# A first-layer product in seven half-block products, masks and bias by accumulating transfers, heads in two pairs: a two-layer graph attention network

## The chip, the cores and the metric

One core of a Trainium2 chip runs the whole kernel. The metric is the device time in microseconds of one execution; every run here is listed as being in the fast state. Before the change the median of the first three runs is 2880.1 us (2879.95 to 2880.22). Ratios of two kernels are the mean time of one kernel's fast runs over that of the other's in the same rounds on the same chip, so they are not quite the ratio of the medians quoted beside them.

## The reference, cut to what matters

32 graphs of 512 nodes with 512 features each. Per graph: normalise and rectify, a first attention layer with four heads of 256 features, ELU, a second layer with one head of 512 features, and the residual.

```python
def gat_layer(x, mask, W, a_src, a_dst, bias, concat):
    xl = (x @ W).reshape(B, N, H, F)
    asrc = jnp.einsum('bnhf,hf->bnh', xl, a_src)
    adst = jnp.einsum('bnhf,hf->bnh', xl, a_dst)
    e = jax.nn.leaky_relu(asrc[:, :, None, :] + adst[:, None, :, :], 0.2)
    e = jnp.where(mask[..., None], e, NEG_INF)
    attn = jax.nn.softmax(e, axis=1)                  # over the sources
    out = jnp.einsum('bsdh,bshf->bdhf', attn, xl)     # the "product over the sources"
    ...
    return out + bias
h = jax.nn.elu(gat_layer(h, mask, W1, att_src1, att_dst1, b1, concat=True))
return x + gat_layer(h, mask, W2, att_src2, att_dst2, b2, concat=False)
```

Each layer is a projection (`x @ W`) and, per head, a product over the sources with the attention weights p.

## The kernel before

All is in fp32. Three of the four large products already use seven half-block products in place of eight: both projections and the second layer's product over the sources. (Two matrices cut into 2 x 2 blocks need eight block products; with sums of blocks made before, and sums of results after, seven are enough.) The first layer's product over the sources is still plain, 4 source tiles of 512 columns for each of 8 blocks of features:

```python
def gather1(b, soft):
    for h in range(H):
        pk, p = soft.p.pop(h)
        for f in range(FPH):
            g = h * FPH + f
            bk, ps = banks.take()
            for s in range(NT):
                v, vkeys = features(b, h, s)
                pe(vkeys + [pk + (s,)], [bk], 0.862,
                   [(mm, (ps, v[:, f * P : (f + 1) * P], p[:, s, :]), ...)])
            act(0.62, ..., e, ps, AF.Exp, bias=b1_sb[:, 0, g : g + 1], scale=-1.0)   # ELU
            act(0.62, ..., e, e, AF.Relu, bias=1.0, scale=-1.0)
            dve(0.67, ..., nc.vector.scalar_tensor_tensor, h1[:, g, :], ps, ...)
```

VectorE makes the logits of p, adds the mask (a large negative number, bf16, in SBUF), and ScalarE exponentiates:

```python
for u in range(NT):                       # Soft.second: one head
    dve(0.67, ..., nc.vector.scalar_tensor_tensor, p[:, u, :], rr[:, 0, :], ...)
    dve(0.59, ..., nc.vector.tensor_add, p[:, u, :], p[:, u, :], m[:, u, :])
    act(0.62, ..., p[:, u, :], p[:, u, :], AF.Exp, bias=z[:, 2, j, u : u + 1])
...
dma(256e3, (), halves, xr, x[b, d * P : (d + 1) * P, :])                  # residual
dve(0.59, [xk, "b2"], halves, nc.vector.tensor_add, xr, xr, b2_sb)        # + bias
```

One thing matters more than it seemed to: no instruction is issued where it stands in the code. Each becomes a job with an assumed cost, what it reads and what it writes, and `Program.order()` works out one fixed order for each engine, and for each queue that issues transfers, from those costs. The program is emitted in that order, and nothing in it changes a list by what really finishes when.

## Time and profile before

| | before |
|---|---|
| time, median | 2880.1 us |
| span of the profiled execution | 2877.3 us |
| TensorE busy | 2842.6 us, 99% |
| VectorE, ScalarE busy | 2469.7 us (86%), 2206.1 us (77%) |
| TensorE idle between 200 and 2700 us | none |
| transfer engines busy | 38% |

These are the groups of instructions that the change touches (line, engine, operation, what it writes and reads, shape and count, then busy us, mean ns of one, and the engine's idle time before them):

```profile
L285 PE MATMUL mm<-p,xl 128*128 128x512 f32 x2016 | 871.4, 592 | 1.6 <-ACT p L274 1.6
L277 DVE TENSOR_TENSOR p<-p,m 128x512 f32<-128x512 f32 x640 | 416.4, 684 | 0.0
L277 DVE TENSOR_TENSOR xr<-xr,b_sb 128x512 f32<-128x512 f32 x124 | 84.2, 684 | 1.0 <-DMA xr<-in_x_dram 1.0
```

The first is the plain product (31 graphs of 64 records, and the last graph's second layer). The other two are VectorE's mask and bias sums, 500 us of its busy time.

### The profile page before, as it was taken

Reading aid. Unit: us, or ns where it says so; the run is one execution under the profiler, and the core shown is the slowest. Engines: PE = TensorE matmul, PEld = TensorE weight load, DVE = VectorE, ACT = ScalarE, POOL = GpSimd, SP = SyncE. Lnnn points to the kernel's source line nnn. Section 1 sums busy time; section 2 is a strip of 40 time slices with the busy share of each in tenths; the row PEclk is TensorE's granted clock in tenths of the full one; section 3 lists DMA queues with packets and bytes.
Section 4 is the critical chain, followed back from the end, with each engine's and each line's share of the span. In section 5 each row is a group of like instructions: output and inputs, shape, how many; then the busy total and the mean of one; then the engine's idle time right before and its main releaser. Section 6 shows DMA issues by size and latency. Waiting matters only on the chain.

```text
span 2877.3 us, 35818 instructions
## 1 busy us (share of the span) xinstructions
PE 2842.6 (99%) x11016; PEld 2091.4 (73%) x11016; DVE 2469.7 (86%) x5979; ACT 2206.1 (77%) x4381; POOL 54.5 (2%) x38
## 2 busy tenths in 40 slices
PE   7899999999999999999999999999999999999999
PEld 6577778777777777787777877777877778777776
DVE  6998899888888888888888888888988888988886
ACT  5878887778877788777888778787787887878872
POOL 0000000000000000000000000000000000000000
PEclk9999999999999999999999999999999999999999
DMA  6333433434333434334333334333343433434322
GB/s 199 91 102 94 128 107 102 119 96 129 106 110 112 119 99 124 103 108 121 103 117 104 109 112 119 105 113 109 107 129 91 126 107 106 123 100 110 114 70 88
DMA packets 323328, 318.71 MB, mean 111 GB/s; under 512 B 219840, under 2 KB 223936, under 8 KB 323136
## 3 DMA queue, kind: packets, MB, share of 16 engines
q1 hardware_dynamic: 323136, 316.42, 37.7%
q8 instruction: 87, 1.43, 0.2%
q14 instruction: 105, 0.86, 0.1%
HBM read 232.53 MB, written 34.54 MB: 93 GB/s over the span
## 4 chain that ended last, share of the span: by engine, by line
PE 97%; DVE 2%; ACT 0%; DMA 0%; issue 0%; SPq 0%; DVEq 0%; ACTq 0%
PE mm L285 97%; DVE p L277 1%; DVE xr L277 0%; DVE l L277 0%; DMA w_sb<-in_L_gnn_W_dram 0%; DVE xl L277 0%; ACT xr L274 0%; DVE h L277 0%; SPq L280 0%; ACT p L274 0%; DVE w_sb L277 0%; ACT ht L274 0%; DVE x L277 0%; DVE stats L277 0%; ACT l L274 0%
## 5 line engine op out<-in xcount | busy, mean ns | idle before, releaser
L285 PE MATMUL mm<-p,xl 128*128 128x512 f32 x2016 | 871.4, 592 | 1.6 <-ACT p L274 1.6
L285 PEld LDWEIGHTS mm<-p,xl 128*128 128x128 f32 x2016 | 382.4, 190 | 472.3 <-issue 413.7
L285 PE MATMUL mm<-w_sb,hs 128*128 128x257 f32 (+1 forms) x3024 | 685.8, 381 | 4.3 <-DVE hs L277 4.3
L285 PEld LDWEIGHTS mm<-w_sb,hs 128*128 128x128 f32 x3024 | 575.2, 190 | 89.5 <-DVE hs L277 4.7
L274 ACT ACTIVATE xl<-mm 128x258 f32<-128x258 f32 (+2 forms) x752 | 286.9, 382 | 420.6 <-PE mm L285 407.4
L274 ACT ACTIVATE l<-l,low 128x512 f32<-128x512 f32 x640 | 456.8, 715 | 114.3 <-DVE low L277 113.6
L274 ACT ACTIVATE p<-p,z 128x512 f32<-128x512 f32 x640 | 433.3, 713 | 72.2 <-DVE p L277 71.5
L285 PE MATMUL mm<-w_sb,h 128*128 128x257 f32 x2056 | 469.5, 380 | 7.5 <-DVE h L277 7.5
L285 PE MATMUL mm<-w_sb,ht 128*128 128x258 f32 x2112 | 475.1, 381 | 1.8 <-DVE xr L277 1.8
L277 DVE SCALAR_TENSOR_TENSOR p<-rr,z 128x512 f32<-128x512 f32 x640 | 456.1, 743 | 20.3 <-DMA rr<-drr 14.5
L285 PEld LDWEIGHTS mm<-w_sb,ht 128*128 128x128 f32 x2112 | 401.2, 190 | 73.1 <-issue 11.0
L274 ACT ACTIVATE l<-as,z 128x512 f32<-128x512 f32 x640 | 438.4, 714 | 12.5 <-DMA as<-das 7.6
L277 DVE CUSTOM_DVE_ANT_1 l<-l,mt 128x512 f32<-128x512 f32 x640 | 426.0, 682 | 14.9 <-ACT l L274 14.7
L285 PEld LDWEIGHTS mm<-w_sb,h 128*128 128x128 f32 x2056 | 390.1, 190 | 66.5 <-DVE h L277 8.3
L277 DVE TENSOR_TENSOR p<-p,m 128x512 f32<-128x512 f32 x640 | 416.4, 684 | 0.0
L277 DVE TENSOR_TENSOR xl<-xl,mm 128x258 f32<-128x258 f32 x558 | 230.3, 418 | 65.4 <-PE mm L285 51.6
L277 DVE SCALAR_TENSOR_TENSOR h<-mm,b_sb,xr 128x512 f32<-128x512 f32 x256 | 187.2, 744 | 110.3 <-ACT xr L274 110.0
L277 DVE TENSOR_TENSOR xr<-mm,xr 128x256 f32<-128x256 f32 (+1 forms) x424 | 172.1, 419 | 25.6 <-PE mm L285 22.3
L285 PE MATMUL mm<-xl,p 128*128 128x256 f32 (+1 forms) x752 | 181.0, 390 | 3.2 <-ACT p L274 3.2
L274 ACT ACTIVATE xr<-mm,b_sb 128x512 f32<-128x512 f32 x256 | 170.5, 675 | 12.3 <-PE mm L285 9.5
L285 PEld LDWEIGHTS mm<-xl,p 128*128 128x128 f32 x752 | 142.5, 190 | 32.0 <-issue 7.5
L274 ACT ACTIVATE ht<-x 128x1024 uint16<-128x1024 uint16 x124 | 159.2, 1341 | 1.2 <-PE mm L285 1.2
(92 smaller groups left out, 1977.6 us busy)
## 6 DMA issues: line engine op xcount, KB each, us to landing
rr<-drr SPq DMA_DIRECT2D x160, 512.0 KB
x<-in_x_dram SPq DMA_DIRECT2D x129, 256.0 KB
adj<-in_adj_dram SPq DMA_DIRECT2D x128, 256.0 KB
as<-das SPq DMA_DIRECT2D x64, 512.0 KB
xr<-in_x_dram SPq DMA_DIRECT2D x124, 256.0 KB
out_dram<-xr SPq DMA_DIRECT2D x124, 256.0 KB
as<-das SPq DMA_DIRECT2D x32, 256.0 KB
drr<-rr SPq DMA_DIRECT2D x160, 4.0 KB
```

Of the source, the lines that this page charges most:

```text
L274: prog.add("ACT", cost, reads, writes, lambda: nc.scalar.activation(*a, **k))
L277: prog.add("DVE", cost, reads, writes, lambda: f(*a, **k))
L285: f(*a, **k)
```

## The change

Its intent is to take an eighth of the last plain product off TensorE. The half-block products need sums of blocks, on VectorE, which has no room for them by the prediction's count (76.3 us busy per graph of 88.2, and 19.1 to be added); so the masks and the bias go to transfers that add to what is in SBUF. The heads go in two pairs with half of the next graph's projection between them, so that three buffers of p are enough. The ordering was reworked as well (12 rounds, each backwards and then forwards, in place of one; transfers now queue up one after another in the backward pass too). The core of the diff, cut:

```diff
-    DMA_LEAD, DMA_TAIL, DMA_RATE = 1.2, 1.0, 230e3
+    DMA_LEAD, DMA_TAIL, DMA_RATE = 1.2, 1.0, 280e3
...
+    ROUNDS = 12
+        for _ in range(self.ROUNDS):
+            back = self.backwards(rank)
+            start, done = self.forwards(late)      # keep the order with the earliest end
...
+    def accumulate(size, reads, writes, to, at, cost=0.95):
+        prog.add("POOL", cost, reads, writes,
+            lambda: nc.gpsimd.dma_start(to, at, accum_op=OP.add), 1.4 * size)
...
+            here = self.b == B - 1 or self.layer == 1 and (h in HERE or self.b == 0 and h < H - 1)
-                dve(0.59, ..., nc.vector.tensor_add, p[:, u, :], p[:, u, :], m[:, u, :])
+            if not here:
+                for us in (0, 1), (2, 3):          # two tiles of p a transfer
+                    accumulate(500e3, keys + [mk], keys, *(... for t in (p, md)))   # md: masks in DRAM
...
+        op(0.34, add, s1, a21, a22)                # sums1: eight block sums of one head
+        op(0.59, sub, t1, b12, b11)
+        op(0.34, sub, s2, s1, a11)
+        op(0.59, sub, t2, b22, t1)
+        op(0.34, sub, s4, a12, s2)
+        op(0.34, sub, a21, a11, a21)
+        op(0.59, sub, b12, b22, b12)
+        # and, before the last product: op(0.59, sub, b21, b21, t2)
...
+            if n in (1, 4, 5, 6):                  # gather1: seven products of a head
+                act(COPY, [bk], [key], to, ps, AF.Copy)
+            else:
+                dve(ADD, [bk, key], [key], nc.vector.tensor_add, to, to, ps)
...
+            accumulate(256e3, [xk], halves, xr, rows_of(b2, P))      # residual: bias
...
+            gather1(s, 0)                          # the loop over graphs
+        s.second(2); s.second(3); ...
+            for _ in range(14):
+                next(ahead)                        # half the projection of graph i + 2
+            gather1(s, 1)
```

Graphs 0 and 1 stay plain (`PLAIN = 1`).

## The prediction

> **What bounds the kernel now.** I first read the page's first and fourth parts, busy time by engine and the chain that ended last.
>
> ```profile
> PE 2842.6 (99%) x11016; PEld 2091.4 (73%) x11016; DVE 2469.7 (86%) x5979; ACT 2206.1 (77%) x4381; POOL 54.5 (2%) x38
> PE 97%; DVE 2%; ACT 0%; DMA 0%; issue 0%; SPq 0%; DVEq 0%; ACTq 0%
> q1 hardware_dynamic: 323136, 316.42, 37.7%
> ```
>
> The tensor engine carries 97% of the chain; VectorE has 14% of the span free, and the transfers use 37.7% of their engines. The table by stretches, cut into three times 88.2 us, says whether that holds inside the steady state and what one graph costs:
>
> ```profile
> 1000.00:1088.20 88.20, 88.20 (x346) 65.15 (x345) 77.94 (x190) 70.10 (x141) 1.01 (x1) 1.00 0.41 117
> 1088.20:1176.40 88.20, 88.20 (x345) 65.16 (x344) 76.55 (x184) 68.74 (x138) 1.38 (x1) 1.00 0.37 111
> 1176.40:1264.60 88.20, 88.20 (x345) 65.17 (x344) 74.34 (x177) 67.34 (x132) 2.58 (x1) 1.00 0.37 111
> ```
>
> Columns after the window: its length, then busy us of PE, weight loads, VectorE, ScalarE, GpSimd, then granted clock and transfer share. Nothing stalls PE: 88.2 of 88.2 us at full clock, 345 matmul records each. The code gives 344 per graph (each fp32 matmul shows as two records): 112 for each of the two projections in seven products, 56 for the second product over sources, 64 of 512 columns for the first. VectorE takes 76.3 us per graph on average, ScalarE 68.7. All the PE waits of the run together are 30.9 us, in the first 165 us and before the very last product; the rest is solid matmul. So only PE's own instruction time counts, as long as the others keep up.
>
> A record's duration (592 ns) is not its cost; matmuls overlap. The cost is the step from start to start, which runs of equal records in the timeline give:
>
> ```profile
> 1379.44 20.76 PE L285 MATMUL mm<-p,xl 128*128 128x512 f32 x48
> 1407.36 5.38 PE L285 MATMUL mm<-w_sb,hs 128*128 128x258 f32 x24
> 2833.60 3.62 PE L285 MATMUL mm<-x,ht 128*128 128x256 f32 x16
> ```
>
> 512 columns: (20.76 - 0.592)/47 = 0.429 us. 256 columns: (3.62 - 0.379)/15 = 0.216. 258: (5.38 - 0.383)/23 = 0.217. Check: 64 x 0.429 + 112 x 0.2175 + 112 x 0.217 + 56 x 0.216 = 88.2 us, the period.
>
> The same must be done for VectorE, whose durations also overlap:
>
> ```profile
> 1399.97 0.68 DVE L277 TENSOR_TENSOR hs<-hs,ht 128x512 f32<-128x512 f32 x1
> 1400.57 0.69 DVE L277 TENSOR_TENSOR ht<-ht 128x512 f32<-128x512 f32 x1
> 1401.17 0.74 DVE L277 SCALAR_TENSOR_TENSOR h<-mm,b_sb,xr 128x512 f32<-128x512 f32 x1
> ...
> 1414.52 0.42 DVE L277 TENSOR_TENSOR xl<-xl,mm 128x258 f32<-128x258 f32 x1 [0.26 <-PE mm L285]
> 1414.86 0.69 DVE L277 TENSOR_TENSOR xr<-xr,b_sb 128x512 f32<-128x512 f32 x1
> ```
>
> A 512-element sum steps by 0.60 us (1399.97 to 1400.57 to 1401.17) though shown as 0.68; a 256-element one by 0.34. ScalarE's copy of a block out of an accumulator, from the same timeline (1409.59 us minus the start before it at 1409.32), steps by 0.27 to 0.28.
>
> [...] 0.429 is 2 x 0.216 less 3 ns, so splitting 512 columns in two costs almost nothing[...]. [...]
>
> **The change part by part.**
>
> *Matmuls removed.* For graphs 2 to 31 (graphs 0 and 1 stay plain) the first product of a head becomes seven half-block products of 2 source tiles by 256 columns: 7 x 2 x 2 records, 112 per graph for four heads, instead of 64 of 512. 64 x 0.429 = 27.46; 112 x 0.216 = 24.19; 3.27 us saved per graph, 30 graphs: 98 us, all on the chain. The period falls from 88.2 to 84.9. If nothing else stalls: 2880 - 98 = 2782. Weight loads: 2091 + 30 x 48 x 0.19 = 2365 us of 2782, 85%, hidden as now.
>
> *VectorE removed, per graph.* Mask sums: 4 heads and the second layer, 4 each, 20 x 0.60 = 12.0. Bias sums into the residual: 4 x 0.60 = 2.4. Together 14.4.
> *VectorE added, per graph.* Block sums of a head: four of 256 elements, four of 512: 4 x 0.34 + 4 x 0.60 = 3.76, four heads: 15.0. Of the seven results of a head three are added by VectorE: 12 x 0.34 = 4.1. Together 19.1. Net +4.7: 76.3 becomes 81.0 us of an 84.9 us period, 95%. So the "masks by transfer" part doesn't speed anything up by itself; it makes room for the sums, and not quite enough.
> *ScalarE.* Four copies per head, 16 x 0.28 = 4.5 per graph; the ELU's exponential reads SBUF instead of an accumulator, eight times, perhaps 0.06 less each by the Relu's step of 0.52 against 0.58. 68.7 becomes 72.7 of 84.9, 86%.
> *GpSimd and transfers.* 608 of the 640 mask sums become 304 transfers (two tiles each), and 124 bias sums become 124; with the author's 0.95 us of issue, 428 are about 400 us on an engine 2% busy. Transfers: 316 MB in 37.7% of 2877 us is 292 GB/s while busy. A mask transfer writes 0.52 MB[...]: 1.8 us if only writes count, about 3.6 us if the read-back counts fully; 304 of them are 550 to 1090 us, so the share rises to 57 to 77%. [...]
> *Order.* Heads come in pairs, with 14 products of the next graph's projection (56 x 0.2175 = 12.2 us) between them. There are three buffers for p: head 2's stands free during the first pair, head 3 must reuse one of the pair's. [...] Half the buffer is released at the last seventh product, 3.4 us before the pair's end, and the sums are wanted only after four products of the next pair. [...]
>
> Sum: 2880 - 98 = 2782 as the floor. What I add is a choice: VectorE at 95% in strict static order won't always deliver block sums, or the add that frees an accumulator (wanted within two to three products of 0.86 us), in time. I allow 0.5 us of PE stall per graph, 16 us in all: 2798. Start and end I leave as they are (about 31 us of waits).
>
> **Rivals.** (1) *VectorE becomes the bound.* For: 95% on average, and the pair stage alone asks 2 x 3.76 + 6 x 0.34 + 4 x 0.67 = 12.2 us of it in 56 x 0.216 = 12.1 us of PE. Against: PE doesn't wait at all at 87%, the order is searched twelve times, and its assumed costs (0.59, 0.34) match the measured steps. If 2 us per graph leak: 2782 + 60 = 2842, within 2%. (2) *The accumulating transfers are late*: the chain gets a transfer of unknown latency where a 0.60 us sum stood. If each takes 9 us[...], head 3's chain misses by perhaps 2 us per graph, again about 2840. For: three p buffers only, and a queue shared with broadcasts. Against: the transfer engines would still be idle a quarter of the time, and today's broadcasts make VectorE wait only 14.5 us in the whole run. (3) *Seven products cost more than six eighths suggest*: if a group of two accumulating matmuls left bubbles, the gain would shrink. Against: the second product already runs such groups of 256 columns, at 0.216 us. (4) *All hidden*: PE stays solid, 2775 to 2785.
>
> **Range and chances.** Faster by over 2% means below 2822.5 us, which leaves 40 us for stalls over the floor, 1.3 us per graph. The author's tuned model and today's solid PE make that likely; the 4 us of VectorE slack makes it uncertain. 2775 to 2838 should hold 8 in 10. Faster 0.80, within 2% 0.17, slower 0.03: for slower the transfers would have to cost 5 us per graph.
>
> **What would show it.** The first product as about 3360 records of 256 columns stepping by 0.216; PE busy about 2745 us in a span near 2795; period 84.9 to 85.5; VectorE 93 to 95%; ScalarE about 85%; transfer share 57 to 77%; p<-p,m sums down to 32. PE waits should name VectorE's block sums or ScalarE's exponentials of p, under 20 us beyond the start. I am wrong if those waits exceed 45 us, if VectorE's busy time falls (then I mis-sized the sums), or if the matmul step is above 0.22.

## The result, and the profile after

The changed kernel takes 2860.94 us in the median (2858.04 to 2869.5, four runs), before 2880.16 on the same chips; the ratio is 0.9937, 95% interval 0.9916 to 0.9959. It gives the right result. It is 0.6% faster, so within 2% of before; 2798 us had been predicted, and 2860.94 lies above the predicted range of 2775 to 2838.

The page after the change, its parts on busy time, the chain and the queues:

```profile
PE 2774.1 (97%) x12456; PEld 2365.5 (83%) x12456; DVE 2584.4 (90%) x6567; ACT 2306.4 (81%) x4861; POOL 416.7 (15%) x466
PE 5%; DVE 4%; ACT 1%; DMA 1%; issue 0%; SPq 0%; DVEq 0%; POOL 0%; ACTq 0%; POOLq 0%
q1 hardware_dynamic: 327600, 332.68, 41.7%
q0 software_dynamic: 61632, 191.92, 30.3%
p<-dm POOLq DMA_DIRECT2D x304, 512.0 KB, 5.1
```

TensorE still leads in busy time, but its share of the chain fell from 97% to 5%: the chain now hops between engines and transfers and could be followed back only to about 2513 us, so its shares cover only the end. The last line gives the mask transfers' median time from issue to landing, 5.1 us. In the table by stretches, the long middle of the two kernels, before and then after:

```profile
200.00:2700.00 2500.00, 2500.00 (x9766) 1850.95 (x9765) 2168.86 (x5195) 1954.79 (x3887) 48.77 (x28) 1.00 0.38 111
```

```profile
200.00:2700.00 2500.00, 2463.33 (x11257) 2131.79 (x11256) 2311.36 (x5831) 2079.82 (x4385) 388.20 (x429) 1.00 0.75 191
```

TensorE was solid for 2500 us and now stands idle for 36.7. The count says more than the busy time. A graph is now 392 records in 84.9 us if nothing stalls, so 11,543 would fit into 2500 us; 11,257 ran. The 286 missing ones, at 84.9/392 = 0.217 us, are 62 us lost. (In before 2500 us hold 9751 records of a period of 88.2 us with 344, and 9766 ran: nothing lost.) A second count agrees: in the trace's records of the middle, the times from start to start exceed the steps by 61 us in all (before: 1.5), 44 of them in 47 waits of over 0.3 us. The step itself did not change; in the timeline of after, 16 records of 256 columns show the same 3.62 us as before:

```profile
1015.12 3.62 PE L333 MATMUL mm<-p,xl 128*128 128x256 f32 x16
1018.57 3.62 PE L333 MATMUL mm<-t,hs 128*128 128x256 f32 x16
```

So the ledger is this. Counting all matmul records by their steps (0.429, 0.2175, 0.217 and 0.216 us for 512, 258, 257 and 256 columns): before 2080, 3600, 3584 and 1736 records, 2828 us; after 160, 3600, 3584 and 5096, 2730 us. The saving is 98 us, as predicted. Everything else took 2877 - 2828 = 49 us before and 2856 - 2730 = 126 us after. Of these 77 us more, 62 lie in the middle, and some 15 at the start and the end.

What TensorE waited for in the middle, from the view of waits (total us, times, longest):

```profile
PE mm L333 <- DVE hs L319: 13.1, 5, 3.6
PE mm L333 <- DVE xr L319: 11.8, 17, 2.3
PE mm L333 <- ACT xl L316: 5.7, 12, 0.9
PE mm L333 <- ACT h L316: 5.0, 6, 1.8
```

Which matmuls they hold up is told by the groups of instructions, over the whole run:

```profile
L333 PE MATMUL mm<-xl,hs 128*128 128x256 f32 x232 | 60.8, 391 | 12.5 <-DVE xr L319 11.8
L333 PE MATMUL mm<-x,hs 128*128 128x256 f32 x464 | 110.3, 393 | 10.8 <-DVE hs L319 10.8
L333 PE MATMUL mm<-p,xl 128*128 128x256 f32 x1920 | 447.8, 381 | 6.4 <-ACT p L316 3.5 <-ACT h L316 2.9
L333 PE MATMUL mm<-t,hs 128*128 128x256 f32 x960 | 218.3, 380 | 1.2 <-ACT h L316 0.9 <-DVE t L319 0.3
L333 PE MATMUL mm<-p,hs 128*128 128x256 f32 x480 | 113.8, 380 | 1.2 <-ACT h L316 1.2
```

The first two are of the second layer's product, which was in seven products before; the last three are the new seven products. So most of the waiting is not in the new products: of the 44 us in the middle, 28 lie in the second layer's product, 10 in the projections and 6 in the new products.

None of the waits names a transfer, and `hs` are the block sums, which look like VectorE's load. One must ask what VectorE waited for in turn. The longest of the five waits for `hs`, in the timeline, line by line (start, length, engine, instruction, in brackets the idle time before it and what ended it):

```profile
446.76 0.86 POOL L327 DMA_DIRECT2D p<-dm  x1 [0.45 <-issue]
...
456.26 1.33 ACT L316 ACTIVATE p<-p,z 128x512 f32<-128x512 f32 x2 [0.99 <-DMA p<-dm]
...
457.63 0.69 DVE L319 TENSOR_TENSOR hs<-p 128x512 f32<-128x512 f32 x1 [1.29 <-ACT p L316]
...
458.38 1.22 PE L333 MATMUL mm<-x,hs 128*128 128x256 f32 x2 [3.63 <-DVE hs L319]
```

The mask transfer issued at 446.76 landed just before 456.26, 9.5 us later; ScalarE idled for it, then VectorE for ScalarE, then TensorE for VectorE. VectorE is the name on the wait, and a transfer stands at its head. But ScalarE idled for the transfer for only 0.99 us, so in this place at most about 1 of TensorE's 3.63 us is shown to be the transfer's. A wait for `xr` runs the same way with a bias transfer at its head, and there the transfer accounts for 2.00 of 2.34 us:

```profile
1159.62 0.42 DVE L319 TENSOR_TENSOR xr<-mm,xr 128x256 f32<-128x256 f32 x1 [2.00 <-DMA xr<-in_L_gnn_b_dram]
...
1160.10 1.13 PE L333 MATMUL mm<-xl,hs 128*128 128x256 f32 x4 [2.34 <-DVE xr L319]
```

In the middle the mask transfers took 4.1 to 9.7 us to land (one of 13.1 us was issued at 158 us, in the start). And the long wait goes with a lower clock: in the 50 us that hold the 3.63 us wait, the granted clock (the figure before the transfer share) is 0.97 where it was 1.00:

```profile
450.00:500.00 50.00, 46.13 (x204) 39.13 (x204) 42.99 (x112) 40.73 (x80) 9.21 (x10) 0.97 0.82 204
```

That is 0.03 x 50 = 1.5 us more. The clock record of this trace has stretches at half clock, single ones of 3.4 us (and 6.8 or 10.2 us at start and end). Four of them lie in the middle, and they go with the waits of 3.63, 3.00, 2.72 and 2.34 us: each begins within 1.3 us of the end of one, and the 16 records there take 5.25, 5.35, 5.41 and 5.30 us where 16 took 3.62. None goes with the wait of 2.29 us that ends at 1469.46. Together the four cost about 7 of the 62 us.

### The profile page after: what moved, and what is told of

Its sections match the earlier page's. It is cut to its first block, busy times and chain, and to the rows that moved or that the text cites. A ratio compares the mean times of both kernels' runs of the same rounds, so it can differ in the third digit from the quotient of the medians.

```text
span 2856.2 us, 41534 instructions
## 1 busy us (share of the span) xinstructions
PE 2774.1 (97%) x12456; PEld 2365.5 (83%) x12456; DVE 2584.4 (90%) x6567; ACT 2306.4 (81%) x4861; POOL 416.7 (15%) x466
## 3 DMA queue, kind: packets, MB, share of 16 engines
q1 hardware_dynamic: 327600, 332.68, 41.7%
q0 software_dynamic: 61632, 191.92, 30.3%
## 5 line engine op out<-in xcount | busy, mean ns | idle before, releaser
L333 PE MATMUL mm<-w_sb,hs 128*128 128x257 f32 (+1 forms) x3024 | 693.2, 383 | 19.4 <-ACT xl L316 10.8
L327 POOL DMA_DIRECT2D p<-dm x304 | 267.5, 882 | 2032.1 <-DVE p L319 1034.3
L333 PE MATMUL mm<-p,xl 128*128 128x256 f32 (+1 forms) x2016 | 489.5, 391 | 6.4 <-ACT p L316 3.5
L333 PE MATMUL mm<-w_sb,ht 128*128 128x258 f32 x2112 | 481.5, 382 | 2.2 <-ACT xl L316 1.2
L319 DVE TENSOR_TENSOR xl<-xl,mm 128x258 f32<-128x258 f32 x558 | 224.8, 417 | 36.6 <-PE mm L333 28.7
L316 ACT ACTIVATE h<-mm 128x256 f32<-128x256 f32 x480 | 175.4, 379 | 84.2 <-PE mm L333 82.0
L316 ACT ACTIVATE xr<-h,b_sb 128x512 f32<-128x512 f32 x240 | 171.5, 723 | 77.3 <-DVE h L319 76.8
L333 PE MATMUL mm<-t,hs 128*128 128x256 f32 x960 | 218.3, 380 | 1.2 <-ACT h L316 0.9
L333 PEld LDWEIGHTS mm<-t,hs 128*128 128x128 f32 x960 | 183.1, 191 | 27.0 <-ACT h L316 1.3
L319 DVE SCALAR_TENSOR_TENSOR h<-h,b_sb,xr 128x512 f32<-128x512 f32 x240 | 175.9, 745 | 20.0 <-ACT xr L316 19.2
```

Of the source, the lines that this page charges most:

```text
L316: prog.add("ACT", cost, reads, writes, lambda: nc.scalar.activation(*a, **k))
L319: prog.add("DVE", cost, reads, writes, lambda: f(*a, **k))
L327: lambda: nc.gpsimd.dma_start(to, at, accum_op=OP.add), 1.4 * size,
L333: f(*a, **k)
```

## The kernel's own plan

Since every engine is given a fixed list, the loss can be split with the builder's own arithmetic: `order()` ends with a planned time for its order. That is a calculation from its cost table, not a measurement; it was read out after the prediction.

```
             planned end   TensorE work in the plan   planned TensorE idle   measured   measured - planned
before         2863.9            2819.9                     44.0              2880.1        16
after          2787.4            2712.8                     74.6              2860.9        74
```

The plan assumes slightly short matmul steps: 2828 - 2820 = 8 us of the excess before and 2730 - 2713 = 17 us after are only that. What remains are stalls that the plan doesn't have: 8 us before, 56 us after. So the 98 us saved were lost in two ways: 31 us because the order that was found already leaves TensorE idle for that much longer, and some 48 us because execution doesn't keep to it. 98 - 31 - 48 = 19, the gain measured.

Two theories for the second loss. **T**: transfers land later than the order assumes (it counts on 5.6 to 9.0 us for a mask transfer, 5.7 in the median). **V**: VectorE, at 90% and more, can't deliver whatever the transfers do.

## The experiments

Each kernel is the changed one with the edit shown (left out: lines that only set up or clear a tile, and `ROUNDS = 40` in e6, e7 and e10). "Middle loss" is worked out as above from the count of matmul records between 200 and 2700 us; after: 62 us. The strongest comparisons are those in which the order of every instruction is the same: the first three against the changed kernel, and e7 against e4.

**e1: small mask transfers, same order.** Wrong result on purpose. (A first form without the constant exponent overflowed in the check before the chip and was not run.)

```diff
-  *(t[:, us[0] : us[-1] + 1].rearrange("p t n -> p (t n)") for t in (p, md)),
+  *(t[:, us[0], :16] for t in (p, md)),
-  p[:, u, :], p[:, u, :], AF.Exp, bias=z[:, 2, j, u : u + 1],
+  p[:, u, :], p[:, u, :], AF.Exp, bias=six[:, u : u + 1], scale=1e-6,    # six: -6.0
```

> Wrong result on purpose. The changed kernel with the same order of every instruction, but each of the 304 accumulating mask transfers moves 16 columns instead of 1024, and the exponentials of p take a constant bias so that nothing overflows. VectorE's work is untouched. Theory T (transfers land later than the fixed order assumes, and the waits reach TensorE): 2790 to 2815 us, the mask transfers land in 2 to 3 us instead of 5.1, ScalarE's waits for broadcasts and masks (177 us now) fall under 60. Theory V (VectorE at 90 to 95% can't deliver the block sums in time whatever the transfers do): 2845 to 2862 us, with the same TensorE waits for block sums and residual adds.

Measured: 2826.62 us (2823.59 to 2829.33), ratio 0.9816. 34 us are gone, more than half of the 56, with VectorE's work unchanged; the mask transfers landed after 2.4 us in the median (2.2 to 5.5). It fell between the two ranges. So the mask transfers cost that much in this order. Not separated: their own landing, and the load that they put on other transfers (the transfer engines fell from 75% to 53% busy in the middle, the bias transfers from 5.8 to 5.3 us). Its middle, and VectorE as busy as ever:

```profile
200.00:2700.00 2500.00, 2481.00 (x11392) 2160.26 (x11391) 2343.04 (x5891) 2109.78 (x4450) 390.27 (x430) 1.00 0.53 132
```

11,392 records: 151 short, 33 us lost instead of 62. The part of the expectation on ScalarE's waits was wrong: its waits for masks vanished (63.2 us in the middle before), but those for the broadcasts of the source scores only fell from 92.8 to 79.8 us.

**e2: small block sums, same order.** Wrong result on purpose.

```diff
-  dve(cost, u[1] + v[1], to[1], f, to[0], u[0], v[0])
+  dve(cost, u[1] + v[1], to[1], f, *(q[0][:, :1, :32] for q in (to, u, v)))
```

> Wrong result on purpose. Same order, same transfers, but the eight VectorE block sums of each head in the seven-product first layer work on 32 columns instead of 256 or 512, which takes about 12 us per graph of 80 off VectorE. Theory V: 2790 to 2810 us, VectorE near 78% busy. Theory T: 2840 to 2860 us, TensorE waits hardly changed, since the broadcasts and masks land as late as before.

Measured: 2859.44 us (2854.96 to 2866.13), ratio 0.9932, no different from the changed kernel.

```profile
200.00:2700.00 2500.00, 2459.13 (x11226) 2129.49 (x11225) 2005.44 (x5808) 2073.56 (x4371) 389.76 (x429) 1.00 0.75 190
```

VectorE fell from 2311 to 2005 us busy in the middle, 10.7 us per graph, and TensorE lost 69 us there instead of 62. V falls as an explanation of the stalls in this order. VectorE was not short of time; it was waiting: in this run its waits for the broadcasts of `rr` rose to 78.2 us, from 31.0.

**e3: small bias transfers, same order.** Wrong result on purpose.

```diff
-  accumulate(256e3, [xk], halves, xr, rows_of(b2, P))
+  accumulate(256e3, [xk], halves, xr[:, :16], rows_of(b2, P)[:, :16])
```

> Wrong result on purpose (bias of layer 2 mostly missing). Same order, but the 124 bias transfers into the residual move 16 columns instead of 512. It asks whether the TensorE waits for residual adds (11.8 us visible, 24.1 at the weight loads) come from late bias transfers. If so: 2830 to 2845 us, those waits nearly gone. If they come from VectorE's backlog or from the masks: 2850 to 2862 us and the waits stay.

Measured: 2852.39 us (2848.59 to 2861.6), ratio 0.991. 8.5 us, with intervals that overlap (0.9892 to 0.9928 against 0.9916 to 0.9959); the waits for residual adds fell only from 11.8 to 8.7 us, at the weight loads from 24.1 to 18.7. By this run bias transfers are at most a small part.

**e4: 40 rounds of ordering instead of 12.** Right result.

```diff
-    ROUNDS = 12
+    ROUNDS = 40
```

> Right result. The order is searched 40 times instead of 12; the program's own plan then ends at 2768.5 us instead of 2787.4 (before: 2863.9 planned, 2880 measured). If the loss is in the plan (order not good enough), the measured time falls by about the same 19 us, to 2835 to 2848. If the loss is in transfers that don't keep the plan, a tighter plan gains little or nothing: 2850 to 2870 us.

Measured: 2820.58 us (2816.79 to 2822.63), ratio 0.9797. The gain of 40 us is twice the plan's 19. The excess over the plan fell too, from 74 to 52 us. Nothing of the work changed; this alone takes the change to about 2% faster than before (the 95% interval, 0.9781 to 0.9814, lies on both sides of 2%, so that verdict is unclear).

```profile
200.00:2700.00 2500.00, 2486.58 (x11423) 2160.70 (x11422) 2338.10 (x5910) 2113.89 (x4462) 397.51 (x430) 1.00 0.76 192
```

**e5: all heads plain.** Right result. One part alone: the transfers and the new order without the seven products.

```diff
-    PLAIN = 1
+    PLAIN = 31
```

> Right result. The change without its seven-product first layer: every head by plain products, but masks and bias by transfers and the new order. Its plan ends at about 2860 us (before: 2863.9 planned, 2880 measured), and VectorE has some 440 us less to do than in before. If late transfers alone are enough to stall TensorE: 2890 us or more. If they stall it only where the order is tight (the pairs with their block sums): 2872 to 2885 us and TensorE solid in the steady state.

Measured: 2891.24 us (2887.69 to 2894.72), ratio 1.0039. The matmuls are those of before and VectorE has 398 us less to do (2071.5 busy, 72%), and yet it is slower than before: 31 us over its plan of 2860.4, where before has 16. It lies in the first range, but its middle is almost solid (2495.73 of 2500 us), so about half of the loss is at the start and the end. Transfers and new order together cost 11 us even where VectorE is 28% idle; which of the two does isn't separated, and 11 us is within what two orders can differ by (e12).

**e6: the planner told of later landings on a faster queue, 40 rounds.** Right result.

```diff
-    DMA_LEAD, DMA_TAIL, DMA_RATE = 1.2, 1.0, 280e3
+    DMA_LEAD, DMA_TAIL, DMA_RATE = 1.5, 1.2, 320e3
```

> Right result. 40 rounds again, but the planner is told that a transfer takes 0.5 us longer to land (lead 1.5 and tail 1.2 instead of 1.2 and 1.0) on a faster queue (320 instead of 280 GB/s). Its plan ends at 2760.8 us. If the stalls beyond the plan come from landings later than planned, an order with longer landings in mind keeps its plan better than the 40-round run did (2820 measured, 2768.5 planned): 2795 to 2812 us. If the queue's rate matters more than the latency, optimism about it costs: 2820 us or more.

Measured: 2846.66 us (2831.61 to 2858.82), ratio 0.9882. It missed the first range and lies in the second: 86 us over the plan, and the widest scatter of all, 27 us between executions of one kernel. Told of a faster queue, the order was kept worst of all; but two settings changed at once, and it is one order.

**e7: e4 with e1's small mask transfers.** Wrong result on purpose; the same order as e4.

> Wrong result on purpose. The small mask transfers of the first run in the 40-round order. If plan and transfers are two separate losses, they add up: 2820 less 15 to 34, so 2786 to 2805 us. If the better order had already absorbed the late transfers: 2812 to 2820 us.

Measured: 2798.73 us (2797.42 to 2800.66), ratio 0.9718. 22 us less than e4, with the same order. The two losses add up in the main: 62 us together, where 34 and 40 alone would make 74. TensorE is nearly solid again, with 45 records short, 10 us:

```profile
200.00:2700.00 2500.00, 2496.01 (x11498) 2178.71 (x11496) 2366.86 (x5951) 2132.28 (x4491) 397.56 (x430) 1.00 0.53 133
```

VectorE is busy 2367 of 2500 us here, 95%, the figure that the prediction had worked out, and TensorE hardly waits.

**e8: e2 with the planner told the small cost, 12 rounds.** Wrong result on purpose.

```diff
-  dve(cost, u[1] + v[1], to[1], f, *(q[0][:, :1, :32] ...
+  dve(0.12, u[1] + v[1], to[1], f, *(q[0][:, :1, :32] ...
```

> Wrong result on purpose. Block sums on 32 columns as in the second run, but the planner is told their true small cost (0.12 us each), 12 rounds. Its plan ends at 2763.3 us instead of 2787.4. The second run showed that less VectorE work in the old order gains nothing. If VectorE's load matters through the order that it leaves room for, this gains the plan's 24 us or more: 2800 to 2838 us. If only transfers matter: 2845 to 2860 us.

Measured: 2843.52 us (2827.77 to 2850.86), ratio 0.9866. Between the two ranges. 17 us are gained where the plan gained 24. (The 0.12 us is a setting of the planner; by e2 a small sum takes about 0.14 us, an estimate: the 15.0 us of block sums per graph less the 10.7 that e2 took off, over 32 sums.) This suggests that VectorE's load does matter, through the order that it leaves room for; it isn't shown, since one new order against another can differ by 13 us (e12) and this kernel's executions by 23. The stalls beyond the plan stay: 80 us over it, with VectorE 80% busy.

**e9: head 0's masks on VectorE, 40 rounds.** Right result.

```diff
-    HERE = ()
+    HERE = (0,)
-    ROUNDS = 12
+    ROUNDS = 40
```

> Right result. 40 rounds, and the masks of head 0 of every graph are added by VectorE again: 60 fewer mask transfers (a fifth of them), 2.4 us more VectorE work per graph. Its plan ends at 2766.2 us, like the 40-round run's 2768.5 (2820 measured). If mask transfers are what breaks the plan (22 us for all of them at 40 rounds): some 4 us less, 2808 to 2819 us. If VectorE's load decides: 2825 us or more.

Measured: 2802.46 us (2798.68 to 2805.55), ratio 0.9734, 95% interval 0.972 to 0.9749. The fastest right version, better than either range, with VectorE at 94% over the whole run (2643.9 us).

```profile
200.00:2700.00 2500.00, 2493.04 (x11466) 2170.03 (x11465) 2413.36 (x6056) 2129.32 (x4485) 344.65 (x373) 1.00 0.70 180
```

**e10: bias on VectorE, 40 rounds.** Right result.

```diff
-            if places[0] is xrs:
-                accumulate(256e3, [xk], halves, xr, rows_of(b2, P))
-            else:
-                dve(0.59, [xk, "b2"], halves, nc.vector.tensor_add, xr, xr, b2_sb)
+            dve(0.59, [xk, "b2"], halves, nc.vector.tensor_add, xr, xr, b2_sb)
```

> Right result. 40 rounds, and the bias is added to the residual by VectorE again, as in before: no bias transfers, 2.4 us more VectorE work per graph, and the residual is there one landing earlier. Plan 2773.9 us. Small bias transfers gained 8.5 us in the 12-round order, so with 5 us of worse plan against it: 2812 to 2822 us. If VectorE's load decides: 2828 us or more.

Measured: 2833.05 us (2829.52 to 2834.51), ratio 0.9838. A miss of the first range: it lies in the one set for "VectorE's load decides", 12 us slower than e4. But it has the same extra VectorE work as e9, which was 18 us faster than e4. So VectorE's load is not what tells these two apart.

**e11: the planner told of a slower queue, 60 rounds.** Right result.

```diff
-    DMA_LEAD, DMA_TAIL, DMA_RATE = 1.2, 1.0, 280e3
+    DMA_LEAD, DMA_TAIL, DMA_RATE = 1.2, 1.0, 260e3
-    ROUNDS = 12
+    ROUNDS = 60
```

> Right result. 60 rounds, and the planner is told a slower queue, 260 instead of 280 GB/s. The plan ends at 2782.8 us, 14 us after the 40-round run's. Told a faster queue, the order lost 26 us against that run though its plan was shorter; if landings later than planned are the cause, this order is kept better, and the excess over the plan falls from 52 us to 30 to 40: 2812 to 2823 us. If the excess has nothing to do with the planner's idea of the transfers: 2830 to 2840 us.

Measured: 2823.22 us (2817.85 to 2826.88), ratio 0.9805. The excess over the plan fell to 40 us, as expected at the range's edge, but the longer plan ate it; nothing gained on e4.

**e12: e9 with 120 rounds.** Right result.

```diff
-    ROUNDS = 40
+    ROUNDS = 120
```

> Right result. The best version so far (masks of head 0 on VectorE, 40 rounds, 2802 us measured, plan 2766.2) with 120 rounds of searching; its plan ends at 2763.4 us. If measured time follows the plan, some 3 us less: 2794 to 2804 us. If the plan is by now below what the transfers let it keep, nothing: 2800 to 2812 us.

Measured: 2815.31 us (2812.23 to 2820.52), ratio 0.9773. A miss, above both ranges: 13 us slower than e9 with a plan 3 us shorter and the same work. This sizes the luck of an order: two orders of the same jobs differ by 13 us for no reason that the plan shows. Differences of that size between experiments with different orders (e9 against e4, e10 against e4) can't be put down to the work moved.

**A check by calculation, made after the runs.** The builder's fixed order can be replayed with the measured time from issue to landing of each of the GpSimd transfers, in place of the assumed one, and all other costs as planned:

```
          planned   with measured masks   with measured masks and biases   measured
after     2787.4         2809.4                    2840.3                   2860.9
e1        2787.4         2787.4                    2809.9                   2826.6
e3        2787.4         2814.1                    2815.1                   2852.4
e4        2768.5         2777.3                    2800.2                   2820.6
e9        2766.2         2775.3                    2795.8                   2802.5
e12       2763.4         2782.3                    2810.3                   2815.3
```

In the changed kernel 245 of the 304 masks landed sooner after their issue than assumed. Counting only those transfers that landed later gives almost the same, 2841.0 us: a late minority delays the order, and early landings don't make up for it. Its difference of 30 us between the changed kernel and e1 is close to the 34 measured. It also sets e12 behind e9, by 14 us, though the plan had it ahead. It fails for e3, where it would gain 25 us and 8.5 were measured; so how much the biases cost stays open.

## Why the prediction was wrong

Point by point, in its own steps.

- *Matmuls removed*: right. The records came as counted (1920 + 960 + 480 = 3360 of 256 columns in the first product), at the predicted step, and the sum of steps fell by 98 us. Weight loads: 2365 predicted, 2365.5 measured, hidden as before (190 ns each, with the step still at 0.216 us). Rival 3 (costlier small products) is refuted by the unchanged 3.62 us for 16 records.
- *VectorE*: right within a per cent. 81.0 us per graph predicted; 2311.36 us in the middle over 11,257/392 = 28.7 graphs are 80.5. As a share of the middle it was 92%, not 93 to 95%, because the graphs took longer.
- *ScalarE*: 72.7 us per graph predicted, 2079.82/28.7 = 72.4 measured. But a term had the wrong sign: the ELU's exponential got longer, not shorter, when it read SBUF, 723 ns where it was 675. I had compared it with a Relu, a different function (627 ns from SBUF in before, where an exponential from SBUF, that of p, took 713). The total came out right all the same.
- *Transfers*: the share was right, 72% of the transfer engines (57 to 77% predicted; the read-back that the upper end counts was not shown). A mask transfer landed after 5.1 us in the median, a bias transfer after 5.8 (3.9 to 8.8); issuing a mask transfer took GpSimd 862 ns in the median (882 in the mean, 1514 at most), where 0.95 us was assumed. What the prediction left out is the spread: in the middle 4.1 to 9.7 us for a mask transfer. By the replay the late ones count in a fixed order, not the median.
- *The step that failed* is the last of the sum, the allowance for waits: "I allow 0.5 us of PE stall per graph, 16 us in all". The middle shows 62 us over 28.7 graphs, 2.2 us per graph, four times as much, and the start and end, left as they were, some 15 us more. The allowance named the right waits, block sums and the adds that free an accumulator, but gave them to VectorE's load, which e2 refutes for this order. And the working on *Order* looked only at head 3 in the new pairs, and that its chain fits was the author's estimate, with a landing time that no trace had shown; the waits stand mostly in the second layer's product (28 of 44 us), whose chain through a mask or a bias transfer was not worked out. The two terms missing from it are the stalls beyond the plan (56 us against 8), of which the mask transfers are 34 by e1, and the idle time in the plan itself, 31 us more than before, which e4 reduced by 19.
- *The sign of being wrong* was waits over 45 us. From 200 us to the end the view of waits names 50 us (36 in the middle), so it showed if all waits are counted; the block sums and exponentials of p, which were expected there, make 24.5 of them, and the adds that free an accumulator, which were not, 11.8.
- *Rival 2* (accumulating transfers late, "again about 2840") came nearest, but not in its terms: the transfers took 5.1 us in the median and not 9 (16 of 304 took over 8), and the queue isn't shared with the broadcasts (q0 and q1 on the page, with 30.3% and 41.7% of the same 16 transfer engines). It had been argued down by the transfers' mean share and by the few waits for broadcasts in the old trace. Those say nothing about new transfers in a chain that ends at TensorE. *Rival 1*, the one taken most seriously, is refuted for the order as shipped by e2: 10.7 us per graph less VectorE work changed nothing. e8 suggests that the load has its part in how good an order can be found. *Rival 4* did not happen.
- The argument "the order is searched twelve times" was counted in favour, and it was the other part of the loss: twelve rounds were too few for the changed program (e4). That could have been read out of the builder, not out of the profile.

What stays open: why two orders with nearly the same plan differ by 13 us (e9, e12; the replay points to how late landings strike each, but takes the landings from the same runs), so how much of e4's 40 us is a better plan and how much a lucky order; and which transfers make the remaining stalls in e4 and e9 (the broadcasts of `as` and `rr` were not tried alone).

## What to carry to other kernels

Here transfers took the place of sums on an engine, and their latency entered the chain: 5.1 us in the median for two tiles of p, where each tile's sum had taken 0.60. By the replay it is the late ones and not the median that delay the fixed order (2841.0 us with the late ones alone, 2840.3 with all); so look at minimum, median and maximum of landing (here 4.1, 5.1 and 13.1 us), and follow a wait back past the engine that it names. Take away one suspect's size while keeping the order the same before blaming a busy engine: here a VectorE at 90% was not what stalled this order. A static order has to be searched anew, and long enough, after a change, and then two orders have to be measured, because the plan didn't rank them.
